# Recurrent layers on one core: seven 512 KB sums per unit as accumulating transfers, and the channel gate one step later

## The chip, the cores and the metric

The kernel runs on one core of one Trainium2 chip. A core has five engines with their own instruction streams: PE (TensorE, matmuls), DVE (VectorE), ACT (ScalarE), POOL (GpSimd) and SP (SyncE, which issues most of the loads). They work side by side and wait for each other through semaphores. Transfers (DMA) are carried out by 16 DMA engines, whichever engine issues them. The metric is the time of one execution on the device in microseconds, as the median of several runs.

## What is computed

Four layers follow each other on a tensor `x` of 4 batches, 512 tokens and 512 channels: a cross attention (layer 0), two recurrent layers (1 and 2, alike in form), and a perceiver-like attention with an MLP (layer 3). The change is in the recurrent layers. Cut to what matters:

```python
xa = ln(x, ln1_w, ln1_b)
sx = concatenate([state_row, xa[:, :-1]], axis=1) - xa      # token before minus token
t = tanh((xa + sx * maa_x) @ maa_w1)                        # five groups of 32
m = einsum('blfd,fdc->blfc', t, maa_w2)                     # mw, mk, mv, mr, mg
xw = xa + sx * (maa_w + mw)                                 # likewise xk, xv, xr, xg
w = exp(-exp(time_decay + tanh(xw @ decay_w1) @ decay_w2))
r, k, v, g = xr @ Wr.T, xk @ Wk.T, xv @ Wv.T, silu(xg @ Wg.T)
# per token: out = r . (faaaa * k v + s);  s = k v + w * s   (32 heads, 16 x 16 state)
x = x + (group_norm(out) * g) @ Wo.T
xc = ln(x, ln2_w, ln2_b)
sxc = concatenate([state_row0, xc[:, :-1]], axis=1) - xc
xk2, xr2 = xc + sxc * fmaa_k, xc + sxc * fmaa_r
x = x + sigmoid(xr2 @ fWr.T) * (square(relu(xk2 @ fWk.T)) @ fWv.T)
```

So each unit of work has seven sums "token plus weighted difference" of full width: five in the first half (w, k, v, r, g) and two in the second (k, r), and one sum at the end that adds the gated product to `x`.

## The kernel before

**Units and groups.** The recurrent layers are cut into 16 units: layer (1, 2) by batch (4) by half of the tokens (256). Channels lie on the 128 partitions in four groups of 256 tokens, so a tile such as `xa`, `sx` or `mix_w` is 128 partitions by 1024 floats (512 KB). A unit has eight groups of the recurrence, and the loop over `g` walks through all 128 of them. Each group is three large instructions on DVE: L802 forms k·v from `vr` (in PSUM) and `o_k`, L809 is the scan over the tokens (`kv` and the decay factors `W`, both in SBUF), and L810 multiplies by r. PE then sums over the state dimension into `py` (L824). The `kv` tile has two buffers and `vr` one.

**Order of the rest.** Everything else of a unit is written as three generators, `mixes`, `outputs` and `channels`. Each `yield step, phase` says at which group, relative to the unit's first one, and in which of the phases EARLY, SOON, MID, LATE the next piece is issued. Within a step, `summed` of the group before and `scan` of the group itself are issued first, then the phases in order; `repeated` (which makes the next `vr`) comes after phase EARLY of every fourth step. This order is taken over as it is on PE, DVE, ACT and POOL. So in the loop four units are in work at once: the mixes of one, the recurrence of another, the outputs and the channel half of the two before.

**The sums.** In `mixes`, ACT puts the token `xa` (a tile with one column more, for the token before) and POOL forms `sx` (L600). DVE forms `mixx` from both (L605), PE and ACT the five factors, DVE multiplies them by `sx` (L653), and POOL adds `xa` (L654; in unit 0 DVE does so). PE then takes `mix_w` into the decay and `mix_k`, `mix_v`, `mix_r`, `mix_g` into the products. In `channels`, POOL forms `sxc` (L920), ACT scales it and POOL adds `xc` (L926), once for `xk` and once for `xr`. At the end POOL adds the gated product to the two tiles of `x` (L967). POOL has other work in each unit too: `ruk` (L741), v·al into `y` (L749), `y` times the gate of g (L885) and the inverse square roots (L79), all in the one order of its stream.

**The channel gate.** At step 26, MID, PE forms two `pv` tiles in PSUM; at 26, LATE, DVE computes (tanh + 1)·`pv` (L964). The PSUM pool from which `pv`, `pr`, `pm` and the like come has three buffers. On PE, `pv` is followed by the matmul of `mix_w` (one buffer), `py`, the two tiles of `o_w`, and `vr`.

Of the kernel before, what the change touches and what calls it, by code (L numbers as in the profile page):

```python
# [8 lines left out]
F32 = mybir.dt.float32  # L9
I32 = mybir.dt.int32  # L10
AF = mybir.ActivationFunctionType
ALU = mybir.AluOpType
# [3 lines left out]
P = 128  # L16
B, L, C = 4, 512, 512
KC = C // P
LT = L // P
HS = 16  # L20
TS = 256
# [9 lines left out]
def tile_xattn_rwkv_perceiver(ctx: ExitStack, tc: tile.TileContext, t: dict, out: bass.AP):  # L31
    nc = tc.nc
# [28 lines left out]
    def load_w(src, name):  # L61
        w = wpool.tile([P, KC, C], F32, tag="w", name=name)
        nc.sync.dma_start(w, src.rearrange("(k p) n -> p k n", p=P))
        return w
# [6 lines left out]
    def mm(ps, pairs):  # L71
        for i, (lhsT, rhs) in enumerate(pairs):
            nc.tensor.matmul(ps, lhsT, rhs, start=(i == 0), stop=(i == len(pairs) - 1))  # L73
# [22 lines left out]
    def psum_tile(shape, name):  # L96
        pool, tag = psum["p"]
        return pool.tile(shape, F32, tag=tag, name=name)
# [356 lines left out]
    def recurrent(lp, ep):  # L455
# [5 lines left out]
        EARLY, SOON, MID, LATE = range(4)  # L461

        mp = sp = pvr = pyp = W = None
# [24 lines left out]
        stT = lp.tile([P, KC, B, 2], F32, name="stT")  # L488
# [40 lines left out]
        def flat(a):  # L529
            return a.rearrange("p a l -> p (a l)")  # L530

        def stats(tag, tiles):
            mv = ep.tile([P, NT, 2], F32, tag="mv_" + tag, name="ln_mv")
            for i, x in enumerate(tiles):
                s6 = ep.tile([P, 6], F32, tag="ln_st", name="ln_st", bufs=4)
                nc.vector.bn_stats(s6, x)
                nc.vector.bn_aggr(mv[:, i, :], s6)
            nm = mv[:, :, 0]
            nc.vector.tensor_scalar(nm, nm, -1.0, None, ALU.mult)
            rstd = inv_sqrt(ep, mv[:, :, 1], NT, 1.0, 1e-5, "rs_" + tag)  # L540
            nc.gpsimd.tensor_tensor(nm, nm, rstd, ALU.mult)
            return nm, rstd

        def scaled(tag, tiles, nm, rstd):
            if mp:
                z = mp.tile([P, NT, C], F32, tag=tag, name="z", bufs=BUFS[tag])
            else:
                z = wpool.tile([P, 2, NT, C], F32, tag="w", name="z0")[:, 0]
            for i, x in enumerate(tiles):
                nc.scalar.activation(  # L550
                    z[:, i], x, AF.Identity, bias=nm[:, i : i + 1], scale=rstd[:, i : i + 1]
                )
            return z

        def turned(z, vec, xa, wi, bi):

            for k in range(0, KC, 2):
                pt = psum_tile([P, 2, NT, P], "ptn")
                for a in range(2):
                    for i in range(NT):  # L560
                        nc.tensor.transpose(pt[:, a, i, :], z[:, i, (k + a) * P : (k + a + 1) * P], ident)
                for a in range(2):
                    nc.scalar.activation(
                        xa[:, k + a, 1:],
                        pt[:, a].rearrange("p i l -> p (i l)"),
                        AF.Identity,
                        bias=vec[:, k + a, bi : bi + 1],
                        scale=vec[:, k + a, wi : wi + 1],
                    )

        st = {}

        def mixes(q):

            li, b, hf = units[q]
# [4 lines left out]
            vec, order = c["vec"], orders[li]  # L580
            d = st[q] = {}
            full = [P, NI, TS]
            xa = lp.tile([P, KC, TS + 1], F32, tag="xa", name="xa")
            tiles = xn[b][hf * NT : (hf + 1) * NT]
            nm, rstd = stats("mix", tiles)
            yield -10, EARLY
            z = scaled("mix", tiles, nm, rstd)
            yield -9, EARLY
            turned(z, vec, xa, V_LN1W, V_LN1B)
            nc.scalar.copy(xa[:, :, 0], stT[:, :, b, 1] if hf == 0 else st[q - 1]["last"])  # L590
            last = d["last"] = ep.tile([P, KC], F32, tag="last", name="last")
            nc.scalar.copy(last, xa[:, :, TS])
            cur = xa[:, :, 1:]
            yield -9, MID
            if mp:
                sx = mp.tile([P, KC, TS], F32, tag="sx", name="sx", bufs=1)
            else:
                both = wpool.tile([P, 2, KC, TS], F32, tag="w", name="sx0")
                sx, mix = both[:, 0], both[:, 1]
            nc.gpsimd.tensor_tensor(sx, xa[:, :, :TS], cur, ALU.subtract)  # L600
            yield (-8, SOON) if q == 1 else (-9, LATE)
            if mp:
                mix = mp.tile([P, KC, TS], F32, tag="mix", name="mixx", bufs=BUFS["mix"])
# [20 lines left out]
            ms = {}  # L624
# [26 lines left out]
            def mixed(pair):  # L651
                for x in pair:
                    nc.vector.tensor_tensor(ms[x], ms[x], sx, ALU.mult)  # L653
                    (nc.gpsimd if q else nc.vector).tensor_tensor(ms[x], ms[x], cur, ALU.add)  # L654

            def product(x):
                dst = d[x] = mp.tile(full, F32, tag="o_" + x, name="o_" + x)
# [54 lines left out]
            dst = d["w"] = mp.tile(full, F32, tag="o_w", name="o_w")  # L712
# [189 lines left out]
        def channels(q):  # L902

            li, b, hf = units[q]
            n = f"L{li}_"
            vec, d = small[li]["vec"], st[q]
            xs = xn[b][hf * NT : (hf + 1) * NT]
            nm, rstd = stats("cx", xs)
            yield 21, EARLY
            z = scaled("cx", xs, nm, rstd)  # L910
            yield 22, EARLY
            xc = mp.tile([P, KC, TS + 1], F32, tag="xc", name="xc", bufs=1)
            turned(z, vec, xc, V_LN2W, V_LN2B)
            nc.scalar.copy(xc[:, :, 0], stT[:, :, b, 0] if hf == 0 else st[q - 1]["lastc"])
            last = d["lastc"] = sp.tile([P, KC], F32, tag="lastc", name="lastc")
            nc.scalar.copy(last, xc[:, :, TS])
            cur = xc[:, :, 1:]
            yield 22, MID
            sx = mp.tile([P, KC, TS], F32, tag="sxc", name="sxc", bufs=1)
            nc.gpsimd.tensor_tensor(sx, xc[:, :, :TS], cur, ALU.subtract)  # L920

            def shifted(name, i):
                dst = mp.tile([P, KC, TS], F32, tag="cx", name=name, bufs=BUFS["cx"])
                for k in range(KC):
                    nc.scalar.activation(dst[:, k], sx[:, k], AF.Copy, scale=vec[:, k, i : i + 1])
                nc.gpsimd.tensor_tensor(dst, dst, cur, ALU.add)  # L926
                return dst

            yield 23, EARLY
            xk = shifted("xk", V_FK)  # L930
            yield 23, LATE
            xr = shifted("xr", V_FR)
            yield 24, MID

            kk = mp.tile([P, KC, TS], F32, tag="cx", name="kk", bufs=BUFS["cx"])
            fk = load_w(t[n + "fWk"], n + "fk")
            for m in range(0, KC, 2):
                pm = psum_tile([P, 2, TS], "pm")
                for a in range(2):
                    mm(pm[:, a, :], [(fk[:, k, (m + a) * P : (m + a + 1) * P], xk[:, k, :]) for k in range(KC)])  # L940
                nc.scalar.activation(kk[:, m : m + 2, :], pm, AF.Relu)
                nc.scalar.activation(kk[:, m : m + 2, :], kk[:, m : m + 2, :], AF.Square, scale=0.5**0.5)
            yield 25, MID
            fr = load_w(t[n + "fWr"], n + "fr")

            rr = flat(xr).rearrange("p (i c) -> p i c", i=NT)
            prs = []
            for lt in range(NT):
                pr = psum_tile([P, C], "pr")
                mm(pr, [(xr[:, k, lt * P : (lt + 1) * P], fr[:, k, :]) for k in range(KC)])  # L950
                prs.append(pr)
            for lt in range(NT):
                nc.scalar.activation(rr[:, lt], prs[lt], AF.Tanh, scale=0.5)
            yield 26, MID
            fv = load_w(t[n + "fWv"], n + "fv")
            pvs = []
            for lt in range(NT):
                ls = slice(lt * P, (lt + 1) * P)
                pv = psum_tile([P, C], "pv")
                mm(pv, [(kk[:, k, ls], fv[:, k, :]) for k in range(KC)])  # L960
                pvs.append(pv)
            yield 26, LATE
            for lt in range(NT):
                nc.vector.scalar_tensor_tensor(rr[:, lt], rr[:, lt], 1.0, pvs[lt], ALU.add, ALU.mult)  # L964
            yield 27, LATE
            for lt in range(NT):
                nc.gpsimd.tensor_tensor(xs[lt], xs[lt], rr[:, lt], ALU.add)  # L967


        first = mixes(0)  # L970
# [323 lines left out]
    with (  # L1294
        tc.manual_schedule(engines={E.PE, E.DVE, E.Activation, E.Pool}),
        tc.tile_pool(name="rl", bufs=1) as lp,
        tc.tile_pool(name="rt", bufs=2) as ep,
    ):
        ahead = recurrent(lp, ep)
        layer0(ahead, ep)  # L1300
        for _ in ahead:
            pass
# [66 lines left out]
```

## Time and profile before

| | us |
|---|---|
| median of 3 runs | 3994.53 (3992.94 to 3994.84) |
| the profiled execution | 3992.84 |
| its span, first to last instruction | 3991.1 |
| PE busy | 3636.8 (91%) |
| DVE busy | 2751.1 (69%) |
| ACT busy | 1967.5 (49%) |
| POOL busy | 1611.6 (40%) |
| recurrent groups | from 765 to about 2,410, their end to 2,530 |
| one steady unit (eight groups) | 104.2 to 105.9 |

The page names instructions by engine and source line, with the tiles written and read, the shapes, the count, the busy time and the mean duration, and after the bar the idle time of the engine ahead of them and what ended it. "PEclk" or the clock column is the share of full speed that was granted to PE; the mean of this execution is 0.948. A busy share is a mean over stages with different limits: in layer 0 and layer 3 PE is nearly always busy, while in the recurrent layers DVE is. All transfers of this kernel are issued by SP; POOL issues none.

### The profile page before, as it was taken

To read this page: it belongs to the slowest core of one execution; us is meant where nothing else is said; L and a number is where in the kernel's file an instruction comes from. 1 tells how busy PE (TensorE), PEld (TensorE's weight loads), DVE (VectorE), ACT (ScalarE), POOL (GpSimd) and SP (SyncE) were. 2 spreads that over 40 slices of the span, in tenths; PEclk is the share of its full clock that TensorE was granted. 3 is DMA by queue.
4 is the path that set the end of the run, shared out by engine and by line. 5 is a ranking of instruction groups with operands and counts; after the bars stand their busy time and mean duration, and the time that the engine had idled before them with its cause. 6 is when DMAs were issued, how large, how long until landed. Compare 5 with 4: busy or idle time off the path is not lost.

```text
span 3991.1 us, 59886 instructions
## 1 busy us (share of the span) xinstructions
PE 3636.8 (91%) x24128; PEld 2109.5 (53%) x24128; DVE 2751.1 (69%) x4036; ACT 1967.5 (49%) x3386; POOL 1611.6 (40%) x804
## 2 busy tenths in 40 slices
PE   9999999878888889898988867789999999999989
PEld 3333333544555555555555534456566566656656
DVE  6777777599999999999999993255544444444341
ACT  5767676444444455544444432255445444544441
POOL 4777777224544444454444433232312221221120
PEclk9999998988899999999999988899999999999999
DMA  4000000111222222222222222300122112212213
GB/s 144 22 22 11 14 14 11 65 53 54 64 85 81 82 91 83 77 85 85 75 79 80 75 74 80 89 15 25 33 77 83 51 51 90 72 37 73 69 59 127
DMA packets 148805, 255.27 MB, mean 64 GB/s; under 512 B 12272, under 2 KB 39024, under 8 KB 146480
## 3 DMA queue, kind: packets, MB, share of 16 engines
q1 hardware_dynamic: 148528, 251.45, 19.9%
q8 instruction: 190, 3.11, 0.3%
q14 instruction: 87, 0.71, 0.1%
HBM read 247.23 MB, written 4.19 MB: 63 GB/s over the span
## 4 chain that ended last, share of the span: by engine, by line
PE 67%; DVE 21%; ACT 5%; POOL 3%; issue 3%; DMA 0%; SPq 0%; DVEq 0%; POOLq 0%; ACTq 0%
DVE kv L809 7%; PE pm L73 7%; PE pv L73 6%; PE pt L1144 6%; PE po L73 6%; PE ph L73 5%; PE psc L242 4%; PE pst L279 4%; PE psc L1104 4%; DVE kv L802 4%; DVE kv L810 4%; PE po L1160 3%; PE po L304 3%; PE pr L73 3%; PE pk L73 3%
## 5 line engine op out<-in xcount | busy, mean ns | idle before, releaser
L1136 POOL TENSOR_SCALAR sc<-sc,rs 128x1024 f32<-128x1024 f32 x256 | 287.6, 1125 | 932.9 <-DVE rs L1135 916.3
L809 DVE TENSOR_TENSOR_SCAN kv<-W,kv 128x2056 f32<-128x2056 f32 x128 | 620.5, 4848 | 9.1
L292 POOL TENSOR_TENSOR aT<-aT,nmT 128x1536 f32<-128x1536 f32 x124 | 428.6, 3461 | 206.3 <-ACT aT L290 182.9
L254 DVE CUSTOM_DVE_ANT_0 sc<-psc,nm 128x512 f32<-128x512 f32 x512 | 354.1, 692 | 147.5 <-PE psc L242 89.8
L810 DVE TENSOR_TENSOR kv<-kv,o_r 128x2048 f32<-128x2048 f32 x128 | 352.1, 2751 | 4.4
L1144 PE MATMUL pt<-ident,sc 128*128 128x128 f32 x2048 | 281.8, 281 | 36.4 <-ACT aT L1149 36.1
L1132 ACT ACTIVATE sc<-sc,mx 128x1024 f32<-128x1024 f32 x256 | 292.0, 1142 | 38.4 <-DVE mx L1114 34.6
L1114 DVE CUSTOM_DVE_ANT_0 sc<-psc,nm,mx 128x512 f32<-128x512 f32 x256 | 179.6, 747 | 173.7 <-PE psc L1104 173.7
L802 DVE TENSOR_TENSOR kv<-vr,o_k 128x2048 f32<-128x2048 f32 x128 | 292.1, 2282 | 2.9 <-PE vr L764 2.9
L1149 ACT COPY aT<-pt 128x512 f32<-128x512 f32 x320 | 173.9, 584 | 241.6 <-PE pt L1144 241.3
L1144 PEld LDWEIGHTS pt<-ident,sc 128*128 128x128 f32 x2048 | 230.3, 143 | 102.2 <-issue 54.5
L290 ACT COPY aT<-pst 128x512 f32<-128x512 f32 x372 | 196.5, 595 | 177.2 <-PE pst L279 176.6
L824 PE MATMUL py<-kv,k 128*32 128x512 f32 x1024 | 155.1, 678 | 118.0 <-DVE kv L810 99.7
L781 ACT ACTIVATE W<-o_w 128x2048 f32<-128x2048 f32 x128 | 245.2, 1915 | 22.6 <-DVE kv L809 22.4
L298 ACT ACTIVATE aT<-aT 128x2048 f32<-128x2048 f32 x128 | 246.7, 1929 | 5.6 <-POOL aT L292 4.9
L73 PE MATMUL po<-l_m,hT 128*128 128x512 f32 x512 | 236.9, 608 | 4.4 <-ACT hT L1230 4.4
L73 PE MATMUL ph<-nT,l_m 128*128 128x256 f32 x1024 | 235.6, 385 | 0.0
L1239 DVE TENSOR_TENSOR x<-po,x 128x512 f32<-128x512 f32 x64 | 44.1, 689 | 265.7 <-PE po L73 265.7
L279 PE MATMUL pst<-q,km 32*128 32x512 f32 x1024 | 206.1, 639 | 9.4 <-DVE mxs L254 5.8
L73 PEld LDWEIGHTS ph<-nT,l_m 128*128 128x128 f32 x1024 | 192.0, 191 | 34.2 <-issue 10.1
L242 PE MATMUL psc<-km,q 32*128 32x512 f32 x1024 | 197.9, 650 | 0.8 <-ACT q L223 0.8
L79 POOL TENSOR_TENSOR gn_rs<-gn_rs,mhalf 128x64 f32<-128x64 f32 x16 | 177.1, 11071 | 39.6 <-DVE gn_rs L78 39.6
(244 smaller groups left out, 6923.9 us busy)
## 6 DMA issues: line engine op xcount, KB each, us to landing
l_m<-in_L_W SPq DMA_DIRECT2D x64, 1024.0 KB, 5.2
L_wk<-in_L_Wk SPq DMA_DIRECT2D x16, 1024.0 KB, 5.4
L_wv<-in_L_Wv SPq DMA_DIRECT2D x16, 1024.0 KB, 5.4
L_wr<-in_L_Wr SPq DMA_DIRECT2D x16, 1024.0 KB, 5.2
L_wg<-in_L_Wg SPq DMA_DIRECT2D x16, 1024.0 KB, 5.4
L_wo<-in_L_Wo SPq DMA_DIRECT2D x64, 256.0 KB, 4.4
L_fk<-in_L_fWk SPq DMA_DIRECT2D x16, 1024.0 KB, 5.3
L_fr<-in_L_fWr SPq DMA_DIRECT2D x16, 1024.0 KB, 5.3
```

Source lines behind the costliest of these rows:

```text
L73: nc.tensor.matmul(ps, lhsT, rhs, start=(i == 0), stop=(i == len(pairs) - 1))
L242: nc.tensor.matmul(psc, d["q"][g][rs, lt * P : (lt + 1) * P], d["km"][rs, a, :], start=True, stop=True, tile_position=(32 * r, 0),)
L254: nc.vector.tensor_tensor_reduce(sc, ps[r], d["nm"][lt], 1.0, -3.0e38, ALU.add, ALU.max, mxs[:, a, lt, c : c + 1])
L279: nc.tensor.matmul(pst, d["km"][rs, a, s * P : (s + 1) * P], d["q2", a][rs, :], start=True, stop=True, tile_position=(32 * r, 0),)
L292: nc.gpsimd.tensor_tensor(w[:, n:, :], w[:, n:, :], nmT[:, None, :].to_broadcast([P, NR - n, L]), ALU.add)
L298: nc.scalar.activation(w, w, AF.Exp)
L802: nc.vector.tensor_tensor(kv[:, :, 1:], vrs[q, e].rearrange("p q f l -> p (q f) l"), d["k"][:, i : i + 1, :].to_broadcast(full), ALU.mult,)
L809: nc.vector.tensor_tensor_scan(flat(kv), flat(W[g % 2]), flat(kv), 0.0, ALU.mult, ALU.add)
L810: nc.vector.tensor_tensor(kv[:, :, :TS], kv[:, :, :TS], d["r"][:, i : i + 1, :].to_broadcast(full), ALU.mult)
L1132: nc.scalar.activation(sc, sc, AF.Exp, bias=mx[:, 1, r : r + 1], scale=-1.0, accum_out=sm[:, r : r + 1])
L1136: nc.gpsimd.tensor_scalar(sc, sc, rs[:, r : r + 1], 0.0, ALU.mult, ALU.add)
L1144: nc.tensor.transpose(pt[:, r, :], scs[r][:, s // LT, s % LT * P : (s % LT + 1) * P], ident)
```

## The change

Four things are done.

- A helper `added(dst, src)` issues from POOL's stream a transfer that adds its source to its destination. It takes the place of the POOL sums of the five mixes (not in unit 0, where DVE still adds), of `xk` and `xr`, and of the final sum into `x`.
- The tiles `xa` and `xc` lose their column for the token before, so that a partition's 1024 floats lie without a gap. The difference is formed by a helper `shift` in two POOL instructions: 255 columns, and the first column against the state or the last column of the unit before. ACT's copy into that first column goes.
- The channel gate moves from step 26, LATE to step 27, EARLY: on DVE it now stands behind the three large instructions of group 27, and still ahead of the statistics of the next channel half. The order on PE is the same as before.
- The order on POOL and SP is otherwise unchanged.

```diff
-                        xa[:, k + a, 1:],
+                        xa[:, k + a],
...
+        def added(dst, src):
+
+            nc.gpsimd.dma_start(dst, src, accum_op=ALU.add)
+
+        def shift(sx, cur, before):
+
+            nc.gpsimd.tensor_tensor(sx[:, :, 1:], cur[:, :, : TS - 1], cur[:, :, 1:], ALU.subtract)
+            nc.gpsimd.tensor_tensor(sx[:, :, 0], before, cur[:, :, 0], ALU.subtract)
...
-            xa = lp.tile([P, KC, TS + 1], F32, tag="xa", name="xa")
+            cur = lp.tile([P, KC, TS], F32, tag="xa", name="xa")
...
-            nc.scalar.copy(xa[:, :, 0], stT[:, :, b, 1] if hf == 0 else st[q - 1]["last"])
...
-            nc.gpsimd.tensor_tensor(sx, xa[:, :, :TS], cur, ALU.subtract)
+            shift(sx, cur, stT[:, :, b, 1] if hf == 0 else st[q - 1]["last"])
...
                     nc.vector.tensor_tensor(ms[x], ms[x], sx, ALU.mult)
-                    (nc.gpsimd if q else nc.vector).tensor_tensor(ms[x], ms[x], cur, ALU.add)
+                    if q:
+                        added(ms[x], cur)
+                    else:
+                        nc.vector.tensor_tensor(ms[x], ms[x], cur, ALU.add)
...
-            nc.gpsimd.tensor_tensor(sx, xc[:, :, :TS], cur, ALU.subtract)
+            shift(sx, cur, stT[:, :, b, 0] if hf == 0 else st[q - 1]["lastc"])
...
-                nc.gpsimd.tensor_tensor(dst, dst, cur, ALU.add)
+                added(dst, cur)
...
-            yield 26, LATE
+            yield 27, EARLY
             for lt in range(NT):
                 nc.vector.scalar_tensor_tensor(rr[:, lt], rr[:, lt], 1.0, pvs[lt], ALU.add, ALU.mult)
             yield 27, LATE
             for lt in range(NT):
-                nc.gpsimd.tensor_tensor(xs[lt], xs[lt], rr[:, lt], ALU.add)
+                added(xs[lt], rr[:, lt])
```

More of the change, by code (lines that the diff above doesn't have):

```diff
@@ L588, in mixes @@
             yield -9, EARLY
-            turned(z, vec, xa, V_LN1W, V_LN1B)
-            nc.scalar.copy(xa[:, :, 0], stT[:, :, b, 1] if hf == 0 else st[q - 1]["last"])
+            turned(z, vec, cur, V_LN1W, V_LN1B)
             last = d["last"] = ep.tile([P, KC], F32, tag="last", name="last")
-            nc.scalar.copy(last, xa[:, :, TS])
-            cur = xa[:, :, 1:]
+            nc.scalar.copy(last, cur[:, :, TS - 1])
             yield -9, MID
@@ L911, in channels @@
             yield 22, EARLY
-            xc = mp.tile([P, KC, TS + 1], F32, tag="xc", name="xc", bufs=1)
-            turned(z, vec, xc, V_LN2W, V_LN2B)
-            nc.scalar.copy(xc[:, :, 0], stT[:, :, b, 0] if hf == 0 else st[q - 1]["lastc"])
+            cur = mp.tile([P, KC, TS], F32, tag="xc", name="xc", bufs=1)
+            turned(z, vec, cur, V_LN2W, V_LN2B)
             last = d["lastc"] = sp.tile([P, KC], F32, tag="lastc", name="lastc")
-            nc.scalar.copy(last, xc[:, :, TS])
-            cur = xc[:, :, 1:]
+            nc.scalar.copy(last, cur[:, :, TS - 1])
             yield 22, MID
             sx = mp.tile([P, KC, TS], F32, tag="sxc", name="sxc", bufs=1)
-            nc.gpsimd.tensor_tensor(sx, xc[:, :, :TS], cur, ALU.subtract)
+            shift(sx, cur, stT[:, :, b, 0] if hf == 0 else st[q - 1]["lastc"])
             def shifted(name, i):
```

## The prediction

> **What bounds the kernel now.** I read the page first, then the stretch with the recurrent layers (765 to 2,530 us), because the change touches nothing else. From the page, the row for the engine totals and the two rows of the scan and the product that follows it:
>
> ```profile
> PE 3636.8 (91%) x24128; PEld 2109.5 (53%) x24128; DVE 2751.1 (69%) x4036; ACT 1967.5 (49%) x3386; POOL 1611.6 (40%) x804
> L809 DVE TENSOR_TENSOR_SCAN kv<-W,kv 128x2056 f32<-128x2056 f32 x128 | 620.5, 4848 | 9.1
> L810 DVE TENSOR_TENSOR kv<-kv,o_r 128x2048 f32<-128x2048 f32 x128 | 352.1, 2751 | 4.4
> ```
>
> GpSimd (POOL) is not the bound; what matters is whom it delays. The means of L809 and L810 hide two populations: in the trace most scans take 4.44 us and most L810 2.29 us, but some take 6.2 and 4.1 to 4.4. The timeline shows why:
>
> ```profile
> 1514.58 3.03 POOL L654 TENSOR_TENSOR mix_w<-mix_w,xa 128x1024 f32<-128x1024 f32 x1 [22.17 <-DVE mix_w L653]
> ...
> 1517.56 2.17 POOL L654 TENSOR_TENSOR mix_k<-mix_k,xa 128x1024 f32<-128x1024 f32 x1
> ...
> 1517.80 6.23 DVE L809 TENSOR_TENSOR_SCAN kv<-W,kv 128x2056 f32<-128x2056 f32 x1
> ```
>
> The scan starts at 1517.80 under a POOL sum that ends at 1519.73, and is 1.8 us too long. Next, busy time over two units of steady work:
>
> ```profile
> 1523.00:1734.00 211.00, 188.05 (x1268) 117.66 (x1268) 197.57 (x113) 104.01 (x205) 97.33 (x38) 0.95 0.27 84
> ```
>
> The columns are window, PE, weight loads, DVE, ACT, POOL, clock, DMA share. DVE leads, but PE has only 11 us of idle time a unit of 105.7 us (the distance of corresponding scans). The waits between 1,100 and 2,300 us (11.35 units) tell what that idle time is:
>
> ```profile
> DVE xr L964 <- PE pv L73: 36.1, 22, 2.7
> ...
> PE py L824 <- DVE kv L810: 45.0, 11, 4.3
> PE var L859 <- ACT sq L854: 31.0, 12, 2.6
> PE pm L73 <- DVE mixx L605: 26.6, 20, 1.8
> ```
>
> And the chain that ended last, for one unit:
>
> ```profile
> 1479.46 7.06 PE pm L73 x16
> 1487.85 4.86 DVE mixx L605 x2
> 1492.75 2.67 PE pm L73 x6
> 1497.80 7.12 PE pm L73 x32
> 1514.19 7.08 PE pr L73 x16
> 1525.44 7.08 PE pv L73 x16
> 1535.61 4.45 DVE kv L809
> ```
>
> The path alternates: DVE from the channel gate (L964, 1532.6) to `mixx` (L605), then PE from there to `pv`, then the gate again. Neither engine alone is the bound, so a gain on one is limited by the other.
>
> **What the Trainium skill says.** "SBUF — State Buffer", section "Who interferes with whom": a VectorE instruction with two SBUF inputs contends with a GpSimd instruction that reads SBUF, and whichever started first keeps the pair. The trace agrees: L809 and L810 read two SBUF tiles and stretch by 1.8 to 2.1 us, L802 (one input in PSUM) stays within 2.275 to 2.286. The same section says that DMA doesn't contend with compute engines; no run so far shows it for accumulating transfers. "DMA: Bandwidth & Descriptors", section "Anatomy of one DMA — SWDGE (gpsimd) path": about 2.0 us plus bytes over 436 GB/s, so an estimate of 3.2 us for 512 KB. It has no rate for accumulation. The trace of before has no GpSimd transfer at all; its 1 MB weight loads land in 5.2 to 5.4 us.
>
> **The change part by part.**
>
> (1) Contention that goes. I added what L809, L810 and L605 take beyond 4.44, 2.29 and 0.47 us in the trace between 837 and 2,430 us: 149 us. 134 of them are in instructions that start under a POOL instruction. By that instruction, the sums that leave: `xk` 25.3, `mix_k` 25.1, the final `x` 13.6, `xr` 12.5, `mix_r` 3.2, together 79.7 us. Those that stay (`y`·gate L885 24.8, `y`=v·al L749 19.9, `ruk` 6.6, `sx` 3.0): 54.3.
> In one steady unit (1,480 to 1,590): `mix_k` delays a scan by 1.8, `x` a scan by 1.1, `xk` L810 by 1.8, `xr` L605 by 1.9. But `sx` (L600) is queued behind `xk` on POOL and will be ready to start when L810 wants to; I let it take over all of `xk`'s 1.8. It then ends before L605 instead of delaying it, and L749 comes after L605 instead of inside it (2.1 us). So DVE gets 1.8 + 1.1 + 1.9 + 2.1 = 6.9 us a unit.
>
> (2) The gate moved one scan later. Before, DVE waits 3.2 us a unit for `pv` (36.1 / 11.35). After, scan 27 (2.28 + 4.44 + 2.29) runs first, and `pv` is long done. What is behind it: the two `pv` banks are two of three PSUM buffers, and the next user is the decay matmul into `o_w` (PE 1535.30), then `vr` (1537.47), which L802 of the next scan reads. So PE now waits for the gate. If DVE comes no earlier than now, the gate ends at 1528.8 + 9.1 + 0.7 = 1538.6 and PE loses 3.3 us. With DVE ahead by part 1, its start is set by `var` (PE 1525.4): 1525.4 + 0.3 + 9.1 + 0.7 = 1535.5, just where PE arrives. I take 0.5 us a unit. Repetition of `vr` must also wait for the preceding L802: 0.3 us, from the same walk through the instructions.
>
> (3) The transfers. A unit has nine: seven of 512 KB, two of 256 KB. Each costs POOL the time to issue it, unknown here; I take 1 us, bounds 0.3 and 3 (the upper is the sum that it replaces, 2.2 to 3.5 us). Their landing is off the path as long as it comes before the first reader. From the start of the sum to that reader the trace gives, in steady units: `mix_w` 17.9, `mix_k` 21, `mix_v` 21.5, `mix_r` 27.7, `mix_g` 11.6, `xk` 17.3, `xr` 26.4, `x` 14 us. I take 4.5 us of landing (the estimate above, more for reading the destination; bounds 3 and 8): hidden everywhere. If that cover were gone, the excess would go one to one to PE. Not covered: `mix_w` in the first three units (3.1 us, PE has 5 to 7 us of slack against DVE there), `xk` of the last unit (2.2 us), and the very last `x`, behind which the first loads of layer 3 start (2529.5 to 2531.7). I charge 2.5 + 2.5 = 5 us.
>
> (4) `shift` is now two POOL instructions: 0.25 us more, twice a unit, on an engine that idles half the time. The two ACT copies of column 0 (0.2 us each) go; ACT is 49% busy. Nothing for either.
>
> (5) What PE allows. PE is busy 94.4 us a unit. Of its waits, `py` on DVE (45.0 / 11.35 = 4.0) and `mixx` (26.6 / 11.35 = 2.3) vanish when DVE runs ahead. Those through ACT (`var` 2.7, `pbc` 0.8, `pmm` 1.1) are loops from PE to ACT and back, and stay. New: 0.5 + 0.3. So the unit becomes 105.7 − 6.3 + 0.8 = 100.2. DVE needs less: 105.7 − 4.1 idle − 6.9 = 94.7. So PE becomes the bound, and of some 10 us that DVE could give (6.9 + 3.2), 5.5 are realised.
>
> **Sum.** Eleven steady units × 5.5 = 60.5; the unit before them (972 to 1,073) 4; the three first ones, where only `mix_k` and `mix_r` go, 6; the unit from 2,233 to 2,332 3; the tail 3 (`x` at 2,380, `xk` at 2,413). Less 5 for part 3. In all 71.5. The profiled execution took 3992.8 us (span 3991.1): 3921. The median of the runs is 1.7 higher: 3923.
>
> **Rivals.**
> A, DVE's whole gain arrives: PE's ACT loops shrink too, since everything upstream is earlier. For it: `pmm` and `pbc` waits partly hang on ACT being held by DVE. Against: `var` follows PE's own `pr` by way of ACT. 105.7 − 9 = 96.7: 11 × 9 + 16 − 5 = 110, 3884.
> B, little gain: issuing transfers costs 2 to 3 us and also holds DVE, or `sx`, `ruk` and L749 move into the places that the sums leave, or the granted clock, 0.95 in this stage, falls as PE gets denser (2% of 94.4 is 1.9 us a unit). Against: the gaps of POOL are wide and what L802 shows. With 1 to 4 us a unit left: 3945 to 3985, say 3965.
> C, slower: accumulating transfers land late. Place: `mix_g` and `xk` before PE; price: each us over the cover, which with DVE ahead is about 17 for `mix_g` (its product moves from 1554.9 to 1547.8 and its reader to 1566) and 14 for `xk`. It turns the sign when the two excesses exceed the 5.5 us, from about 18 us of landing. At 22 us: 5 + 8 − 5.5 = 7.5 us a unit, 4080. For it: no trace prices accumulation, and every transfer also reads what it writes. Against: 18 us would be over three times what the double size takes from HBM.
> D, the sums are not the cause of the long scans, and only the gate matters: then PE pays its 3.3 us for DVE's 3.2, and the time stays at 3990. The timeline speaks against it.
>
> **How the numbers follow.** Forecast (3895 to 3945) 0.58, A 0.12, B 0.15, C 0.11, D 0.04. No change is what lies within 0.2%, 8 us, about what this measurement can tell. Faster: forecast, A, and nearly all of B: 0.84. Same: D and a rest of B: 0.05. Slower: C: 0.11. The range goes from A's value to the end of B: 3884 to 3985, leaving out C, D and a part of A.
>
> **What would show it.** Scans and L810 after the sums at 4.44 and 2.29; L809's mean near 4.55 (only `ruk` and L749 left), L810's near 2.55; L605 without the 2.4 us instances. The wait of L964 for `pv` gone, and a new one of PE for L964 of about 0.5 us. Units of 100 us. PE's waits for L810 and L605 nearly gone, DVE waiting for PE at L836, L900 and the gate of `o_g`. No PE wait on a transfer in steady units. If PE waits for transfers, C; if scans are still stretched under POOL's issues, B. The prediction is wrong at its root if PE keeps its waits for DVE although the scans are short.

## The result, and the profile after

The changed kernel takes 3970.86 us (median of 4 runs, 3968.25 to 3974.81) against 3994.07 us (3992.94 to 3994.84): a ratio of 0.9943 [0.9926, 0.996], so 23 us less. Forecast were 3923 us, 71.5 us less. The sign and the wide range (3884 to 3985) were right. The likeliest case (3895 to 3945) was missed: the gain came in at a third of its size.

The profiled execution spans 3973.1 us (3974.8 in all, the slowest of the four runs). First the page's rows that answer to those shown of before: the engine totals, the scan (L819, before L809) and the product after it (L820, before L810).

```profile
PE 3633.5 (91%) x24128; PEld 2111.5 (53%) x24128; DVE 2645.5 (67%) x4036; ACT 1966.5 (49%) x3354; POOL 1386.3 (35%) x836
L819 DVE TENSOR_TENSOR_SCAN kv<-W,kv 128x2056 f32<-128x2056 f32 x128 | 585.3, 4573 | 9.1
L820 DVE TENSOR_TENSOR kv<-kv,o_r 128x2048 f32<-128x2048 f32 x128 | 322.4, 2519 | 4.4
```

DVE did get its time back: the means fell from 4848 to 4573 ns and from 2751 to 2519 ns, and DVE is busy for 106 us less. PE's busy time hardly differs. Next, busy time by stretch, one line for each of two steady units (from one unit's first scan to the next one's). The columns are window and its length, then PE, weight loads, DVE, ACT and POOL, the granted clock, the DMA share and GB/s.

```profile
1899.00:2001.50 102.50, 92.93 (x619) 58.33 (x618) 92.50 (x57) 50.65 (x95) 34.82 (x22) 0.97 0.48 124
2105.70:2212.80 107.10, 96.29 (x620) 59.89 (x619) 92.53 (x57) 50.65 (x95) 34.84 (x22) 0.92 0.45 115
```

DVE is busy for 92.5 us in both (before: 100.5 in the mean). Yet one unit takes 102.5 us and the other 107.1, which is more than before's mean of 105.5. PE's busy time goes with the granted clock. The mean of the eleven steady units is 104.4 us, and figures "a unit" below are such means.

Where the 18.0 us between the two spans come from (scan starts of units 0, 3, 14 and 15, before and after):

| stretch | before | after | difference | forecast |
|---|---|---|---|---|
| up to the first scan | 767.1 | 769.4 | +2.3 | 0 |
| units 0 to 2 | 306.1 | 294.9 | −11.2 | −10 |
| eleven steady units | 1160.0 | 1148.4 | **−11.6** | **−60.5** |
| unit 14 | 98.9 | 100.5 | +1.6 | −3 |
| from unit 15's scan to the end | 1659.1 | 1659.9 | +0.8 | +2 |

Nearly all of the shortfall is in the steady units and the one after them. What PE waits for there, 1,100 to 2,200 us (10.5 units; in all, times, longest), after, the four largest:

```profile
PE var L869 <- ACT sq L864: 25.8, 10, 2.6
PE ptn L561 <- DVE o_g L701: 22.7, 11, 2.1
PE vr L774 <- DVE kv L812: 22.6, 11, 2.1
PE pm L73 <- DVE xr L972: 15.2, 9, 2.7
```

The two waits of before for L810 and `mixx` (4.1 and 2.4 us a unit) are gone. Three others have come: for the gate of g (L701, 2.1 us), for L812 by way of `vr` (2.1 us) and for the moved channel gate (L972, 0.9 to 2.7 us, mean 1.5). So 6.5 us go and 5.6 come. The waits of DVE in the same stretch have the largest new one:

```profile
DVE o_g L701 <- ACT o_g L686: 60.1, 11, 5.5
DVE y L846 <- PE py L834: 22.7, 11, 3.3
```

DVE is ready for the gate of g 5.4 us before ACT has written `o_g`. Why ACT is late, the timeline of after tells. The rows below are its answers for ACT, POOL, DVE and PE, one engine after the other (start, duration, instruction, idle time ahead and what ended it).

```profile
1561.98 2.06 ACT L892 ACTIVATE y<-y,L_gn 128x256 f32<-128x256 f32 x4
1566.52 0.60 ACT L686 ACTIVATE o_g<-pm 128x512 f32<-128x512 f32 x1 [2.47 <-POOL y L895]
...
1564.12 2.36 POOL L895 TENSOR_TENSOR y<-y,o_g 128x1024 f32<-128x1024 f32 x1 [10.55 <-ACT y L892]
...
1567.15 1.28 DVE L701 SCALAR_TENSOR_TENSOR o_g<-o_g,pm 128x512 f32<-128x512 f32 x2 [5.43 <-ACT o_g L686]
1568.35 2.28 DVE L812 TENSOR_TENSOR kv<-vr,o_k 128x2048 f32<-128x2048 f32 x1
...
1567.89 0.66 PE L561 MATMUL ptn<-ident,z 128*128 128x128 f32 x4 [2.02 <-DVE o_g L701]
1570.69 2.09 PE L774 MATMUL vr<-o_v,vsel 32*128 32x512 f32 x8 [2.14 <-DVE kv L812]
```

Read it from the top. `o_g` has two buffers. ACT's tanh (L686) for the coming unit writes the tile that POOL's product `y`·gate (L895) of an earlier unit still reads, so it waits 2.47 us for POOL. POOL starts when ACT has scaled `y` (L892, until 1564.04). Behind the tanh stands DVE's gate (L701). It frees the PSUM banks of g's product, of which the pool has three and which `ptn` needs next: PE waits 2.02 us. L812 is queued on DVE behind L701, and `vr` (one buffer) waits another 2.14 us for L812.

The trace of before had the same chain. Its timeline, ACT and then DVE:

```profile
1577.13 1.08 ACT L676 ACTIVATE o_g<-pm 128x512 f32<-128x512 f32 x2 [2.46 <-POOL y L885]
...
1574.94 4.31 DVE L810 TENSOR_TENSOR kv<-kv,o_r 128x2048 f32<-128x2048 f32 x1
1579.17 1.27 DVE L691 SCALAR_TENSOR_TENSOR o_g<-o_g,pm 128x512 f32<-128x512 f32 x2
```

The 2.46 us were on ACT, off the path, as DVE was still in L810 until 1579.25. (What stretched this L810 by 2.0 us was the same POOL product, 1574.76 to 1577.11, which is not one of the sums that leave.) The first half of `o_g` was ready at about 1577.7, only 1.5 us before DVE came for it.

### The profile page after: what moved, and what is told of

It reads as the page before. It is cut to its first block, busy times and chain, and to the rows that moved or that the text cites. A ratio compares the mean times of both kernels' runs of the same rounds, so it can differ in the third digit from the quotient of the medians.

```text
span 3973.1 us, 60030 instructions
## 1 busy us (share of the span) xinstructions
PE 3633.5 (91%) x24128; PEld 2111.5 (53%) x24128; DVE 2645.5 (67%) x4036; ACT 1966.5 (49%) x3354; POOL 1386.3 (35%) x836
## 4 chain that ended last, share of the span: by engine, by line
PE 67%; DVE 19%; issue 7%; ACT 3%; POOL 3%; DMA 1%; SPq 0%; DVEq 0%; POOLq 0%; ACTq 0%
PE pm L73 10%; DVE kv L819 6%; PE pt L1152 6%; PE po L73 6%; PE ph L73 6%; PE pv L73 5%; PE psc L242 4%; PE pst L279 4%; DVE kv L812 4%; PE psc L1112 4%; PE po L1168 3%; PE po L304 3%; PE pk L73 3%; DVE kv L820 2%; PE pr L73 2%
## 5 line engine op out<-in xcount | busy, mean ns | idle before, releaser
L819 DVE TENSOR_TENSOR_SCAN kv<-W,kv 128x2056 f32<-128x2056 f32 x128 | 585.3, 4573 | 9.1
L820 DVE TENSOR_TENSOR kv<-kv,o_r 128x2048 f32<-128x2048 f32 x128 | 322.4, 2519 | 4.4
L812 DVE TENSOR_TENSOR kv<-vr,o_k 128x2048 f32<-128x2048 f32 x128 | 292.4, 2284 | 24.5 <-PE vr L774 24.5
L834 PE MATMUL py<-kv,k 128*32 128x512 f32 x1024 | 145.2, 637 | 57.1 <-DVE kv L820 38.4
L1168 PEld LDWEIGHTS po<-aT,v 128*32 128x32 f32 x4096 | 103.1, 114 | 169.2 <-ACT aT L1157 84.3
```

The lines of the kernel that those rows point to most:

```text
L812: nc.vector.tensor_tensor(kv[:, :, 1:], vrs[q, e].rearrange("p q f l -> p (q f) l"), d["k"][:, i : i + 1, :].to_broadcast(full), ALU.mult,)
L819: nc.vector.tensor_tensor_scan(flat(kv), flat(W[g % 2]), flat(kv), 0.0, ALU.mult, ALU.add)
L820: nc.vector.tensor_tensor(kv[:, :, :TS], kv[:, :, :TS], d["r"][:, i : i + 1, :].to_broadcast(full), ALU.mult)
```

## The experiments

The theory after the result: the contention went as forecast, and the steady units are now set by PE and by loops from PE over ACT, POOL and DVE back to PE, above all the one over `o_g`, and by the gate's hold on PSUM. The rivals: POOL's transfers cost the time (issue, landing), or DVE still sets the pace.

### One half of the change alone

The gate alone, on the kernel before:

```diff
-            yield 26, LATE
+            yield 27, EARLY
```

> The kernel before with nothing changed but the channel gate, moved from step 26 LATE to step 27 EARLY; all sums stay on POOL. Theory of the loops (a wait of DVE for pv is exchanged for waits of PE for the gate, because the two pv tiles hold two of three PSUM buffers): no change to speak of, 3985 to 4003 us, and PE shows a wait for the gate before the o_w matmul of 2.5 to 3.5 us a unit. Rival (the gate's move is what made the changed kernel faster, since it takes away 3.2 us of DVE waiting a unit): 3955 to 3972 us.

Measured: 4075.95 us, 1.0205 [1.0189, 1.022]. Both expectations missed; the kernel is slower by 82 us. A unit takes 112.7 us. PE's waits, 1,100 to 2,200 us (about 9.8 units), cut:

```profile
PE pm L73 <- DVE xr L964: 57.6, 9, 6.5
...
PE vr L764 <- DVE kv L802: 21.4, 10, 2.1
PE ptn L561 <- DVE o_g L691: 20.9, 10, 2.4
PE pm L73 <- DVE mixx L605: 17.1, 10, 1.7
```

The kind of wait that part 2 named is there (the decay matmul into `o_w` waits for the gate), but at 6.4 us rather than 3.3. The waits for L812's counterpart and for the gate of g come up here too, without any transfer. In place of DVE waiting for `pv`, PE waits for the gate and then DVE for `vr`. PE's idle time rises from 11.3 to 16.8 us a unit, and its busy time by 1.7 us, with a clock of 0.93 where before had 0.95. Together these are the 7.3 us by which the unit grows.

The transfers alone, which is the changed kernel with the gate where it was:

```diff
-            yield 27, EARLY
+            yield 26, LATE
```

> The changed kernel with the gate back at step 26 LATE: the transfers and the shift alone. Theory of the loops: in the changed kernel PE waits 0.9 to 2.7 us a unit for the moved gate and DVE has more than 10 us to spare, so putting it back takes some 1.5 us off a unit: 3948 to 3962 us; DVE waits for pv, PE no longer for the gate. Rival (the two parts need each other: without the move DVE waits for pv again and the gain goes): 3980 us or more.

Measured: 3954.56 us, 0.9898 [0.9882, 0.9915], as expected. The gate's move costs the changed kernel 16 us. A unit takes 102.6 us, and this line stands for nearly all of them:

```profile
1684.40:1786.76 102.36, 92.75 (x619) 58.15 (x618) 92.49 (x56) 50.58 (x95) 36.04 (x22) 0.97 0.49 124
```

Of the 1.8 us a unit to after's 104.4, only 0.4 are waits of PE (9.7 against 10.1 us idle); 1.4 are PE's busy time (92.9 against 94.35), with the clock at 0.97 in all units but one. After's best units (102.5 us, clock 0.97) equal these. That the moved gate costs time is shown; that it does so mostly by way of the clock is a reading of two kernels.

What the clock follows can be read from the traces. It has two values only, full and half, and changes only on a grid of 3.41 us, whose intervals are called clock windows here. The waits for `ptn` and `vr` after show a change (the columns are those of the stretches above):

```profile
1567.21:1570.62 3.41, 0.66 (x4) 0.42 (x4) 3.41 (x3) 3.41 (x6) 3.41 (x3) 1.00 0.46 177
1570.62:1574.03 3.41, 3.34 (x10) 1.32 (x11) 3.38 (x2) 3.38 (x10) 0.18 (x1) 0.50 0.00 0
```

In the steady units of all fourteen profiles, PE idled for more than 2 us in 186 clock windows, and each is followed by one at half clock; no window at full clock follows one with more than 1.97 us of idle time. So waits of PE that are long, or stand close together, cost a second time. After has 18 of these idle windows and 35 at half clock (of 336), the transfers alone 13 and 23 (of 329). What brings on the other windows at half clock is not shown, and no run changed the clock alone.

### Are the transfers themselves to blame?

All nine sums of a unit left out, with the gate at 26, LATE:

```diff
-            nc.gpsimd.dma_start(dst, src, accum_op=ALU.add)
+            pass
```

> Shift as in the changed kernel, the gate at step 26 LATE, and the nine sums of a unit left out of the result altogether, neither on POOL nor as transfers. Theory that the transfers are hidden: the same time as with them (3954.6 us), 3940 to 3960 us, the lower end because of the first readers in the first three units and at the end. Rival (the transfers cost something in every unit, by the time to issue them or by landing late): 3935 us or less.

Measured: 3945.08 us, 0.9877 [0.986, 0.9893]. The steady units are those of the transfers alone, 102.6 us and the same waits to a tenth:

```profile
PE vr L774 <- DVE kv L812: 23.6, 11, 2.1
PE ptn L561 <- DVE o_g L701: 21.0, 11, 1.9
PE py L834 <- DVE kv L820: 12.8, 11, 1.2
```

So in steady units the transfers cost nothing, neither by their issue nor by their landing. The 9.5 us come after unit 15's first scan (1649.1 us to the end against 1659.8), and there between the last scan and the first attention matmul of layer 3: 138.3 us against 148.6, while the rest takes 1431 us in both. In this stretch PE waits 3.8 us instead of 10.3 for the last unit's `xk`, and 11.2 instead of 14.9 for the first load of layer 3. With the sums on POOL, in the kernel before, the two waits are 7.2 and 10.8 us. So at the end, where nothing covers them, the transfers do cost time.

The five mixes back on POOL, the rest as transfers, gate at 26, LATE:

```diff
-                    if q:
-                        added(ms[x], cur)
-                    else:
-                        nc.vector.tensor_tensor(ms[x], ms[x], cur, ALU.add)
+                    (nc.gpsimd if q else nc.vector).tensor_tensor(ms[x], ms[x], cur, ALU.add)
```

> Only the sums of xk, xr and x as transfers, with shift; the five mix sums stay on POOL and the gate at step 26 LATE. Theory that what counts is which DVE instruction a POOL sum holds up: mix_k delays a scan by 1.8 us a unit just ahead of the pv wait, where PE is as late as DVE, so leaving the mixes on POOL costs little and most of the 39 us is kept: 3955 to 3970 us. Rival (each sum is worth its share of the contention, half of it is the mixes'): 3970 to 3980 us.

Measured: 3962.6 us, 0.992 [0.9905, 0.9935], as expected. The steady unit is again 102.4 us; the 8 us to the transfers alone lie in units 0 to 2 (309.1 against 299.8 us). For a steady unit it is enough that `xk`, `xr` and `x` leave POOL: DVE is busy for 94.6 us a unit instead of 92.5, and yet the unit doesn't get longer.

### Is PE the bound?

The product of k over half of its contraction, in the changed kernel and in the one before:

```diff
-[(perm(wx[:, k], i + a), ms[x][:, k, :]) for k in range(KC)]
+[(perm(wx[:, k], i + a), ms[x][:, k, :]) for k in range(KC if x == "r" else KC // 2)]
```

> The changed kernel with the product of k over two of its four channel groups only, which leaves half of k out of the result; PE has 3.9 us a unit less to do in a place where it waits for nobody. Theory that PE is now the bound: nearly all of it is gained, 3.0 to 3.9 us a unit, 3922 to 3940 us. Rival (the loops through ACT, POOL and DVE set the pace, PE's work is cover for them): PE waits longer elsewhere and the time stays above 3960 us.

> The kernel before with the product of k over two of its four channel groups only, which leaves half of k out of the result: the same 3.9 us of PE work a unit less that brought the changed kernel from 3971 to 3915. Theory that before, the path runs over DVE at this place and has moved to PE with the change: nothing to speak of, 3982 to 3998 us, and PE waits that much longer for L810. Rival (PE set the pace there in both kernels): 3935 to 3950 us.

Measured: in the changed kernel 3914.66 us, 0.9801 [0.9786, 0.9816], 56 us less than it, more than expected. The unit falls by 4.3 us for 4.1 us of PE's busy time, with its waits nearly as they were (9.8 against 10.1 us). In the kernel before 3986.97 us, 0.998 [0.9974, 0.9987], as expected: the steady units stay at 105.5 us, and PE's waits for DVE grow by what it was given:

```profile
PE py L824 <- DVE kv L810: 55.0, 20, 4.9
PE py L824 <- DVE y L836: 28.8, 11, 2.6
```

So at this place the path did pass from DVE to PE.

### Is it the loop over `o_g`?

POOL multiplies `y` by itself, so that it no longer reads `o_g` and nothing waits for it there; shown for after, and made for before and for the transfers alone as well:

```diff
-            nc.gpsimd.tensor_tensor(y, y, d["g"], ALU.mult)
+            nc.gpsimd.tensor_tensor(y, y, y, ALU.mult)
```

> The changed kernel, but POOL multiplies y by itself instead of by the gate of g; this leaves the gate out of the result, with the same instruction shape and the same two SBUF reads. What goes is one dependence: ACT's tanh of a new g no longer waits for POOL to have read the old one. Theory of the loops (the wait for POOL's product holds back ACT's tanh, then DVE's gating of g, then PE's transposes and vr): PE's wait of 2.0 us a unit before ptn goes and the one before vr halves, about 3 us a unit, 3930 to 3945 us. Rival (PE is simply the bound and these waits are slack that reappears elsewhere): 3962 us or more.

> The kernel before, but POOL multiplies y by itself instead of by the gate of g (the gate is left out of the result), so that ACT's tanh of a new g doesn't wait for POOL. Theory of the loops: before the change DVE was the late one at this place, so nothing is gained: 3985 to 4000 us. Rival (the wait of ACT for POOL cost as much before, so that it is no part of why the gain was small): 3965 to 3975 us.

> Transfers and shift, the gate at step 26 LATE, and POOL multiplying y by itself (the gate of g is left out of the result): both things that held back the changed kernel taken away. Theory that the moved gate (16 us, from 3971 to 3955) and the loop over POOL's product (25 us, from 3971 to 3945) are separate: they add up, 3925 to 3937 us. Rival (they are two faces of one wait, and when one goes the other holds): 3942 to 3955 us.

Measured: after 3945.29 us (0.9878 [0.9864, 0.9893]), 26 us less than the changed kernel, just above the expectation; before 3990.18 us (0.9994 [0.9985, 1.0002]), as expected; transfers alone 3914.45 us (0.9801 [0.9784, 0.9817]), 40 us less than with the loop and more than was expected for the two effects side by side. The wait of `ptn` is gone in the first and third, and the unit is 102.1 and 99.3 us. So the loop costs nothing clear of noise before the change, and taking it away gains 26 to 40 us after it. Part of the gain is clock. In the transfers alone, 2.0 of the 3.3 us a unit are idle time of PE and 1.4 busy time (clock 0.98 for 0.965). In the changed kernel only 0.4 of the 2.3 us are idle time, as a wait of 1.6 us for L820 takes the place of that for `ptn`; 2.0 are busy time (clock 0.968 for 0.948). Clock windows with more than 2 us of idle time fall from 18 to 2 there, and those at half clock from 35 to 21. So the number came near the expectation, but less by shorter waits than by the faster clock. The halving of the wait for L812 that I had expected didn't come in after (1.8 us), but did come near without the gate's move (1.3 us).

The same by issuing the scaling of `y` and POOL's product earlier, in the transfers alone:

```diff
-            yield 14, EARLY
...
-            yield 27, EARLY
+            yield 26, LATE
```

> Transfers and shift with the gate at step 26 LATE, and in the outputs ACT's scaling of y and POOL's product with the gate issued at 13 LATE instead of 14 EARLY, right behind DVE's product; nothing is left out of the result. Theory of the loops: POOL's product is done before ACT comes to the tanh of the new g, PE's wait of 1.9 us before ptn goes: 3925 to 3942 us. Rival (ACT reaches the decay factors and the evacuation of ptn 2.3 us later, and PE waits for PSUM instead): 3952 us or more.

Measured: 3964.52 us, 0.9926 [0.9911, 0.9941]; missed, and 10 us worse than leaving it. The timeline of that kernel, DVE and then POOL:

```profile
1554.20 6.67 DVE L819 TENSOR_TENSOR_SCAN kv<-W,kv 128x2056 f32<-128x2056 f32 x1
1560.90 3.79 DVE L820 TENSOR_TENSOR kv<-kv,o_r 128x2048 f32<-128x2048 f32 x1
...
1554.17 2.40 POOL L894 TENSOR_TENSOR y<-y,o_g 128x1024 f32<-128x1024 f32 x1 [1.35 <-ACT y L891]
1557.88 4.66 POOL L577 TENSOR_TENSOR sxc<-xc 128x1020 f32<-128x1020 f32 x1 [1.31 <-ACT xc L563]
```

The wait for the gate of g does vanish, but POOL's product now begins 0.03 us before the scan, which takes 6.67 instead of 4.44 us, and `sxc` then stretches L820. PE waits 4.1 us for L820 instead. (The time is that of the rival, but not its mechanism.) One loop was exchanged for a contention like those that the change had removed. PE's idle time is about the same (9.4 us a unit for 9.7); what makes the unit 0.8 us longer is its busy time, at a clock of 0.952 instead of 0.965.

A third buffer for `o_g`, paid for with one of `o_v`'s two, without and with the gate's move (shown: without):

```diff
-                dst = d[x] = mp.tile(full, F32, tag="o_" + x, name="o_" + x)
+                dst = d[x] = mp.tile(full, F32, tag="o_" + x, name="o_" + x, bufs={"g": 3, "v": 1}.get(x, 2))
...
-            yield 27, EARLY
+            yield 26, LATE
```

> Transfers and shift, the gate at step 26 LATE, and the tile of g with three buffers instead of two, paid for by one instead of two for v (whose last reader is a step ahead of its next writer); nothing is left out. ACT's tanh then writes a tile that POOL finished with a unit earlier. Theory of the loops: as with y multiplied by itself (3914.5 us), since that is the only dependence that the two kernels take away: 3908 to 3925 us. Rival (that kernel was fast because POOL reads one tile less, not because ACT no longer waits; or v's single buffer makes ACT wait for vr): 3940 us or more.

> The changed kernel, gate at 27 EARLY, with three buffers for g and one for v; nothing is left out. Theory of the loops: the 25 us that y multiplied by itself took off the changed kernel, 3938 to 3952 us. Rival (POOL's second operand is what counted): 3962 us or more.

Measured: 3926.62 us, 0.9829 [0.9815, 0.9844], just above its expectation, and 3933.02 us, 0.9844 [0.9829, 0.9859], better than its expectation (38 us less than the changed kernel). PE's main waits in the first, 1,100 to 2,200 us:

```profile
PE py L834 <- DVE kv L820: 26.4, 22, 1.2
PE vr L774 <- DVE kv L812: 14.4, 11, 1.3
```

No wait for the gate of g, a unit of 99.9 us, and a kernel that computes everything and is 67 us under before and 44 us under the change. Since it multiplies `y` by g as before, what counts is the wait for POOL's product, and not what POOL reads.

## Why the prediction was right and wrong

**The failing step** is the sum in part 5, "New: 0.5 + 0.3. So the unit becomes 105.7 − 6.3 + 0.8 = 100.2", with the 0.5 and 0.3 from part 2. What vanishes was sized well (6.3; measured 6.5). What comes in its place was not (0.8; measured 5.6): the wait for the gate of g, which the sum had at nothing, is 2.1 us, that for `vr` 2.1 for the 0.3 taken, that for the channel gate 1.5 for the 0.5 taken. Means of the eleven steady units:

| PE a steady unit, us | before | after | transfers alone | three `o_g` buffers |
|---|---|---|---|---|
| wait for L810/L820 (`py`) | 4.1 | – | 1.2 | 2.4 |
| wait for `mixx` | 2.4 | – | – | – |
| wait for the gate of g (`ptn`) | 0.1 | 2.1 | 1.9 | – |
| wait for L802/L812 (`vr`) | 0.2 | 2.1 | 2.1 | 1.3 |
| wait for the channel gate | – | 1.5 | – | – |
| waits through ACT | 4.5 | 4.5 | 4.5 | 4.5 |
| busy | 94.2 | 94.35 | 92.9 | 91.75 |
| unit | 105.5 | 104.4 | 102.6 | 99.9 |

I had counted the waits that hang on DVE's lateness as wholly DVE's. Behind the wait of 4.2 us for L810 stood a second condition, the `o_g` chain through ACT and POOL, which left DVE only 1.5 us to gain. The line that tells it, ACT waiting 2.46 us for POOL's `y`, is in the trace of before, on an engine that I had passed over as 49% busy. The signs named DVE waiting for the gate of `o_g`, but the sum didn't ask who then waits for DVE. One unit of before had already shown the outcome (columns as above):

```profile
1601.43:1705.59 104.16, 94.24 (x623) 59.00 (x622) 95.47 (x57) 51.50 (x106) 48.48 (x19) 0.95 0.26 81
```

There POOL's product stands behind L810 instead of ahead of it. DVE is busy for 5.5 us less than in the unit ahead, but the unit is only 1.5 us shorter (104.2 for 105.7): waits of 1.5 us for `ptn` and 1.7 us for `vr` have come. The experiments on `o_g` show this term: nothing before, 26 us (POOL's read left out) to 38 us (third buffer) in the change, 40 and 28 us without the gate's move. The two ways of taking it away don't agree on its size, and why they don't stays open.

**Part 2** was right that the gate would make PE wait for PSUM, and too low: 1.5 us on average for the 0.5 taken, and on the old kernel 6.4 for the 3.3 of its worst case. It also didn't ask what was queued behind the gate on DVE. For `vr` it had 0.3 us from order alone; 2.1 are measured, as L812 stands behind L701, which is late; with L701 in time (three buffers) 1.3 remain.

**Part 5's other input**, a clock of 0.95, held for the changed kernel as a mean (0.948, with 0.92 to 0.97 by unit), but not for the others: it was 0.98 in the version with three buffers. There the unit comes out at 99.9 us, close to the forecast's 100.2, with some luck: PE's matmuls are faster (2.4 us less busy than before), and PE still waits 8.2 us, not the 5.8 that the forecast left it.

**Part 1** was right in the main: 6.9 us a unit forecast, 8.0 measured; means of 4.55 and 2.55 us forecast, 4.57 and 2.52 measured. `sx` took `xk`'s place as expected (L820 of 3.99 us at 1575.14). Two terms were missed that nearly offset each other: `y`·gate no longer stretches L810 (2.0 us), as DVE is past it by then, and v·al into `y` now stretches a scan (1.1 us: 5.59 at 1482.53). Of the 149 us of excess nearly all, not 134, start under a POOL instruction; the sum rests on the figures of one unit, which stand. The trace agrees with the Trainium skill's "SBUF — State Buffer", "Who interferes with whom": whichever instruction comes first holds the pair of ports and the other waits, which the early product of `y` shows by 0.03 us.

**Part 3** was right on the steady units: issue 0.85 to 1.05 us (taken: 1), landing 4.6 to 6.3 us for 512 KB and 4.3 us for 256 KB (taken: 4.5), all hidden, and the version without sums shows the price to be nothing. The 5 us charged for the ends were too little: in after PE waits 10.3 us for the last `xk` where before waited 7.2, and 15.7 for the first load of layer 3 where before waited 10.8, 8.0 us more in all. The estimate of 3.2 us from the Trainium skill's "DMA: Bandwidth & Descriptors", "Anatomy of one DMA — SWDGE (gpsimd) path" is too low for these transfers (4.6 to 6.3 us); the measurement decides. **Part 4** was right that nothing shows in the time, but the second instruction of `shift` takes 2.0 us for `sx`, not 0.25.

**The rivals.** A is excluded, since PE doesn't let DVE's gain through. B's time (3945 to 3985) came true, but not by its mechanisms: no scan is stretched by an issue, the transfers' issue costs a steady unit nothing, and what moved into the places of the sums left DVE more than was forecast (8.0 us for 6.9). Its third, a clock that falls as PE gets denser, is the wrong way round: PE is busy for 85% of the unit at a clock of 0.93 (gate alone) and for 92% at 0.98 (three buffers). C is excluded by the landing times. D is excluded by the scans; its half, "PE pays its 3.3 us for DVE's 3.2", would have been 3990 and measured 4076 on its own. The forecast's own test, that PE keeps its waits for DVE although the scans are short, came true in sum: 6.8 us before, 5.6 after, on other instructions.

## What to carry to other kernels

When an engine is relieved, don't strike out the waits for it: look, for each one, which condition ends last once the engine is early, and read the short waits of the engines off the path (here ACT's 2.5 us for POOL), because these chains are the next bound. Where PE's waits are long or close together, count the clock window at half speed that follows as well. A tile that is written for one unit while an engine still reads it for another ties three engines together through its buffer count, and one buffer more was worth more here (28 and 38 us) than the whole change (23 us). A step moved behind long instructions keeps its inputs' buffers that much longer: price it at the consumer of the buffers, and for what is queued behind it.

## What the runs showed of the hardware

- A transfer that adds SBUF to SBUF costs POOL 0.85 to 1.05 us to issue and lands after 4.3 us (256 KB) or 4.6 to 6.3 us (512 KB). It leaves DVE's long instructions alone: DVE's busy time (92.5 us a unit) and the steady units (102.6 us) are the same with and without such transfers.
- A tiny POOL instruction can be as dear as a large one if it comes behind a DVE instruction with two inputs in SBUF. In after, the first column of `sx` takes ten times what that of `sxc` does, by position alone: it ends 0.07 us after the L820 that it meets. With three buffers it is the other way round in most units, 0.2 us for `sx` and 4.3 for `sxc`, which meets a scan. The groups of POOL in after:

```profile
L578 POOL TENSOR_TENSOR sx<-last,xa 128x4 f32<-128x4 f32 x8 | 16.1, 2014 | 0.0
L578 POOL TENSOR_TENSOR sxc<-lastc,xc 128x4 f32<-128x4 f32 x8 | 1.6, 204 | 0.0
```

- PE's busy time goes inversely with the granted clock: in the four kernels of the table above, busy time a unit times mean clock is 89.4 to 89.9 us, at clocks of 0.948 to 0.980. Of the 4.6 us between after's units at 0.97 (102.5 us) and 0.92 (107.1 us), 3.4 are busy time.
- The granted clock has the values 1 and 0.5 and changes on a grid of 3.41 us. Each of the 186 clock windows with more than 2 us of PE idle time is followed by one at half clock.
- Many steady units last a whole number of clock windows: 102.4 us or 30.0 windows in the transfers alone, 105.8 or 31.0 before, 112.7 or 33.0 with the gate alone, 99.0 or 29.0 in the transfers alone without the loop over `o_g`. In after the unit times repeat every four units, which are 416.5 us or 122.0 windows. That the grid sets the unit is not tested.
